# A four-layer image kernel: in layer 0, the first two turns of a block's attention weights are issued directly behind the next block's scores

## The chip, the cores and the metric

The kernel runs on one core of a Trainium2 chip. The core has five engines that work at the same time, each through its own list of instructions: TensorE (PE in the profile, with its weight loads shown apart as PEld), VectorE (DVE), ScalarE (ACT), GpSimd (POOL) and SyncE (SP), which here only issues DMAs. The metric is the device time of one execution in microseconds, lower is better; the median of three runs before the change is 3686.7 us (3686.67 to 3689.1).

## The reference

Four layers follow each other on 4 images of 64 x 64 points with 128 channels, in 32-bit floats. Layer 0, the only one that is touched, is neighbourhood attention: every point attends, in 4 heads of 32 channels, to the 7 x 7 points around it (shifted inward at the borders), with a learned bias for each relative place. The result is projected, multiplied by a gate that is computed from the input, and added to the input.

```python
qkv = (x @ qkv_w + qkv_b).reshape(B, H, W, 3, HEADS, HEAD_DIM)
q = qkv[..., 0, :, :] * HEAD_DIM ** (-0.5)
...
scores = jnp.einsum('bxyhd,bxyklhd->bxyhkl', q, kwin) + bias[None]
attn = jax.nn.softmax(scores.reshape(B, H, W, HEADS, k * k), axis=-1)
...
out = jnp.einsum('bxyhkl,bxyklhd->bxyhd', attn, vwin).reshape(B, H, W, C)
return out @ proj_w + proj_b
...
gate = jax.nn.sigmoid(jax.nn.relu(x @ g1_w + g1_b) @ g2_w + g2_b)
return attn_out * gate + x
```

Layer 1 is a group normalisation with full attention over the 4096 points, layer 2 a gated product with a layer normalisation, layer 3 a convolution with a selective scan in four directions. None of them is changed.

## The kernel before, in words

The images go through layers 0 to 2 one after the other (the loop over b at L1134). For each image the generator `layer_0` (L359) runs its whole loop before `layer_1` starts, since layer 1 begins with statistics over the image; only its first eight steps (the first two chunks of the intake) are taken during layer 1 of the image before. Layer 3 follows at the end.

An image is cut into 32 blocks (NT) of 8 x 16 points, that is 128 points each. The keys that a block can reach are a rectangle of up to 14 x 22 points: nk is 14 x 19 = 266 for the blocks at the left and right border and 14 x 22 = 308 for the others, or 209 and 242 in the first and the last row of blocks. A block goes through these steps, each a small function:

- `score(i)` (L448): SP loads the block's values; TensorE multiplies queries and keys, one matmul for each head (L477, 32 rows of the array each), into four banks of PSUM. VectorE adds the bias and takes the maximum, head by head (L481), and turns the sign of the maxima (L484). Then `bias_in(i)` (L438) lets GpSimd add the projection's bias times the gate to the block's input (L441, L442).
- `soften(i, heads)` (L490): ScalarE takes the exponential of two heads and their sums (L495).
- `normalise(i)` (L499): VectorE takes the reciprocal of the four sums (L501), GpSimd multiplies the weights of each head by it, in place (L503).
- `by_key(i, g, evac)` (L506): TensorE turns one third of the block's weights so that the keys stand on the partitions: one transpose for each head (L512) into one PSUM bank with the tag "t", and one engine copies the bank to SBUF (L514). Thirds 0 and 2 are copied by ScalarE, third 1 by VectorE. Border blocks of the first and the last row have two parts instead of three.
- `value(i)` (L517): TensorE multiplies the turned weights with the values, a matmul for each third and head (L523, 32 columns of the array each); ScalarE copies the result (L528).
- `project(i)` (L530): TensorE multiplies with the projection's weights (L533); VectorE multiplies by the gate and adds to the input (L534).

Three other things are spread over the loop. `take_in(n, part)` (L377) is the intake of a chunk of four blocks: part 0 finishes the gate of the chunk before (L424 to L426) and turns the input (L387, copied at L389), part 1 computes the queries (L393, L394), part 2 the keys (L400, L401), part 3 values and gate (L411 to L420). `hand_on(n)` (L428) turns four finished blocks for layer 1, also through a bank with the tag "t" (L432), and ScalarE copies it (L433). `statistics(n)` (L435) follows one iteration later on VectorE. "t" has two banks, which are taken in turn by the thirds of `by_key`, by part 0 of the intake and by `hand_on`.

The loop (L543) is a software pipeline: one iteration i issues the scores of block i+3, the values of block i-1, the normalising of block i+1, the projection of block i-2, the turns of block i and the exponentials of block i+2. Instructions that stand in `pin(...)` keep their written order on their engine; those are all of TensorE, VectorE and ScalarE in this loop. The GpSimd operations (L441, L442, L503) and the loads of values on SP are not pinned: their place in their engine's list is set by the planner, which puts there what its plan finds ready first. In the trace the four `bias_in` of a chunk run together on GpSimd, as soon as that chunk's gate is ready.

Of the kernel before, what the change touches and what calls it, by code (L numbers as in the profile page):

```python
# [32 lines left out]
NT = L // P  # L33
# [105 lines left out]
def layers_0_to_2(  # L139
    ctx, tc, xf, mata, matb, rows, rpb, convw, sel, ident, cl, dram, big, ring, early, x3_d, ub_d, zf_d, y_d, dbl_d, ct_d, gw_d, bw_d  # L140
):
    nc = tc.nc
# [10 lines left out]
    def ps_t(shape, name):  # L153
        return psp.tile(shape, F32, name=name, tag="t", bufs=2)
# [31 lines left out]
    def load_x(b, xt=None, tiles=(0, NT), queue=nc.sync, kept=False):  # L186
        if xt is None:
            xt = ring([P, NT, C], f"x_{b}")
        src = xf[b].rearrange("(r w) c -> r w c", w=W)
        for j in range(*tiles):  # L190
            r, c = BR * (j // 4), BC * (j % 4)
            ins = queue.dma_start(xt[:, j, :], src[r:r + BR, c:c + BC, :])
            if kept:

                tc.keep_in_program_order(ins)
        return xt
# [162 lines left out]
    def layer_0(b, xt, edge_t):  # L359
# [12 lines left out]
        def pin(ins):  # L372
            return tc.keep_in_program_order(ins)
# [54 lines left out]
        def hand_on(n):  # L428

            pt = ps_t([P, 4, P], "pt")  # L430
            for k in range(4):
                pin(nc.tensor.transpose(pt[:, k, :], xt[:, 4 * n + k, :], ident))  # L432
            pin(nc.scalar.copy(hT[:, bass.ts(n, CH)], pt.rearrange("p k t -> p (k t)")))  # L433

        def statistics(n):  # L435
            pin(nc.vector.bn_stats(st[:, n, :], hT[:, bass.ts(n, CH)]))
# [53 lines left out]
        def soften(i, heads):  # L490
            k = blocks[i]
            if heads[0] == 0:
                k.sm = sml.tile([P, HEADS], F32, name="sm0", tag="sm0", bufs=4)
            for h in heads:
                pin(nc.scalar.activation(  # L495
                    k.pr[:, h], k.pr[:, h], AF.Exp, bias=k.mx[:, h:h + 1], accum_out=k.sm[:, h:h + 1]
                ))

        def normalise(i):  # L499
            k = blocks[i]  # L500
            pin(nc.vector.reciprocal(k.sm, k.sm))  # L501
            for h in range(HEADS):
                nc.gpsimd.tensor_scalar(k.pr[:, h], k.pr[:, h], k.sm[:, h:h + 1], 1.0, ALU.mult, ALU.mult)  # L503
            k.prT = []

        def by_key(i, g, evac):  # L506
            k = blocks[i]
            if g < len(k.tiles):
                at, n, _ = k.tiles[g]
                pt = ps_t([P, HEADS, P], "pt0")  # L510
                for h in range(HEADS):
                    pin(nc.tensor.transpose(pt[0:n, h, :], k.pr[:, h, at:at + n], ident))  # L512
                prT = tmp.tile([P, HEADS, P], F32, name="prT0", tag="c512", bufs=9)
                pin(evac(prT[0:n], pt[0:n]))  # L514
                k.prT.append(prT)

        def value(i):  # L517
            k = blocks[i]
            po = ps_o([P, P], "po0")
            for g, (at, n, slot) in enumerate(k.tiles):  # L520
                for h in range(HEADS):
                    hp = slice(HD * h, HD * h + HD)
                    pin(nc.tensor.matmul(  # L523
                        po[hp, :], lhsT=vs[0:n, slot, hp], rhs=k.prT[g][0:n, h, :],
                        start=(g == 0), stop=(g == len(k.tiles) - 1),
                    ))
            k.oT = tmp.tile([P, P], F32, name="oT0", tag="oT")
            pin(nc.scalar.copy(k.oT, po))  # L528

        def project(i):  # L530
            k = blocks.pop(i)
            pp = ps_o([P, C], "pp0")
            pin(nc.tensor.matmul(pp, lhsT=k.oT, rhs=m("proj"), start=True, stop=True))  # L533
            pin(nc.vector.scalar_tensor_tensor(xt[:, i, :], pp, gate[:, i:i + 1], xt[:, i, :], ALU.mult, ALU.add))  # L534
# [8 lines left out]
        for i in range(-3, NT + 5):  # L543
            if i + 3 < NT:
                score(i + 3)
            if b == 0 and i < 1:
                load_x(0, xt, (4 * i + 28, 4 * i + 32), kept=True)
            if 0 <= i - 1 < NT:
                value(i - 1)
            if 0 <= i + 1 < NT:  # L550
                normalise(i + 1)
            if 0 <= i - 2 < NT:
                project(i - 2)
            if 0 <= i < NT:
                by_key(i, 0, nc.scalar.copy)
                by_key(i, 1, nc.vector.tensor_copy)
            if 0 <= i + 2 < NT:
                soften(i + 2, (0, 1))
            n, part = divmod(i + 3, 4)
            if n + 2 < NCH or (n + 2, part) == (NCH, 0):  # L560
                take_in(n + 2, part)
            if 0 <= i < NT:
                by_key(i, 2, nc.scalar.copy)
            if 0 <= i + 2 < NT:
                soften(i + 2, (2, 3))

            n, part = divmod(i - 6, 4)
            if 0 <= n < NCH and part == 0:
                hand_on(n)
            if 0 <= n < NCH and part == (1 if n < NCH - 1 else 0):  # L570
                statistics(n)
# [211 lines left out]
    def front(b):  # L783
# [343 lines left out]
        return turn  # L1127

    coming = layer_0(0, x_next, edge_of[0])
    for _ in range(8):  # L1130
        next(coming)
    weights()
    ahead = [x_next]
    for b in range(B):  # L1134
# [26 lines left out]
        if b + 1 < B:  # L1161
            coming = layer_0(b + 1, ahead[0], edge_of[b + 1])
# [385 lines left out]
```

## Time and profile before

| | before |
|---|---|
| median of three runs | 3686.7 us |
| the profiled execution | 3685.77 us |
| its span, first to last instruction | 3684.0 us, mean granted clock 0.920 |
| busy over the span: PE, PEld, DVE, ACT, POOL | 3322.1, 2753.6, 2834.4, 2677.1, 1419.6 us |
| scores of layer 0 (L477), by image | 25.0 to 179.1, 768.9 to 898.9, 1513.2 to 1643.1, 2257.4 to 2387.5 us |
| turns (L512), mean of a matmul, count | 276 ns, 1472 |
| values (L523), mean of a matmul, count | 278 ns, 2944 |
| copies of turned thirds (L514) | ScalarE 240 of 578 ns, VectorE 128 of 686 ns |
| normalising (L503) | 512 of 495 ns on GpSimd |
| exponentials (L495) | 512 of 517 ns on ScalarE |

A group's line in the profile gives line, engine, operation, written and read tiles, shapes, and then busy time, mean duration, and the idle time of the engine just before, with what ended it. In a timeline a row is a run of equal instructions: its start, its length, the engine, and in square brackets the idle time before it and what ended that. "issue" stands for time in which the engine waited for nothing that the profile shows. Times in a timeline are microseconds from the start of the span. Layer 0's loops take about 600 us of the 3684; the rest belongs to the other layers.

### The profile page before, as it was taken

Reading aid. Unit: us, or ns where it says so; the run is one execution under the profiler, and the core shown is the slowest. Engines: PE = TensorE matmul, PEld = TensorE weight load, DVE = VectorE, ACT = ScalarE, POOL = GpSimd, SP = SyncE. Lnnn points to the kernel's source line nnn. Section 1 sums busy time; section 2 is a strip of 40 time slices with the busy share of each in tenths; the row PEclk is TensorE's granted clock in tenths of the full one; section 3 lists DMA queues with packets and bytes.
Section 4 is the critical chain, followed back from the end, with each engine's and each line's share of the span. In section 5 each row is a group of like instructions: output and inputs, shape, how many; then the busy total and the mean of one; then the engine's idle time right before and its main releaser. Section 6 shows DMA issues by size and latency. Waiting matters only on the chain. (4 is left out here: it accounts for less than half of the span.)

```text
span 3684.0 us, 69605 instructions
## 1 busy us (share of the span) xinstructions
PE 3322.1 (90%) x26458; PEld 2753.6 (75%) x26458; DVE 2834.4 (77%) x5325; ACT 2677.1 (73%) x4355; POOL 1419.6 (39%) x1592
## 2 busy tenths in 40 slices
PE   7999999999999999999999999989999997666647
PEld 4679999966899999667999996679999962222236
DVE  5757878767678788776777886767878768999968
ACT  4855677777676777786777777866777769999934
POOL 6500011245122122451222223512222338999866
PEclk8999999999999999999999999999999995555579
DMA  4200000131010012410121213100101269999998
GB/s 123 73 4 28 9 18 33 55 96 31 18 48 29 33 46 84 132 36 18 44 67 33 76 54 94 39 1 27 44 28 35 67 186 236 217 232 212 209 277 283
DMA packets 189394, 310.91 MB, mean 84 GB/s; under 512 B 23007, under 2 KB 111996, under 8 KB 184156
## 3 DMA queue, kind: packets, MB, share of 16 engines
q1 hardware_dynamic: 146260, 220.27, 17.8%
q0 software_dynamic: 24384, 76.95, 11.7%
q10 hardware_dynamic: 18416, 9.24, 0.9%
q8 instruction: 208, 3.41, 0.4%
q14 instruction: 126, 1.03, 0.1%
HBM read 167.69 MB, written 155.56 MB: 88 GB/s over the span
## 5 line engine op out<-in xcount | busy, mean ns | idle before, releaser
L634 PE MATMUL sc<-qT,kT 128*128 128x128 f32 x8192 | 1084.2, 276 | 15.6 <-DVE mx L640 15.6
L667 PE MATMUL po<-v,st 128*128 128x129 f32 x8192 | 1082.1, 275 | 2.0 <-ACT st L661 2.0
L634 PEld LDWEIGHTS sc<-qT,kT 128*128 128x128 f32 x8192 | 1001.4, 193 | 38.4 <-issue 26.6
L667 PEld LDWEIGHTS po<-v,st 128*128 128x128 f32 x8192 | 999.6, 192 | 4.7 <-ACT st L661 2.2
L637 ACT COPY st<-sc 128x512 f32<-128x512 f32 x1024 | 574.0, 583 | 426.9 <-PE sc L634 425.9
L640 DVE TENSOR_TENSOR mx<-mx,sc 128x512 f32<-128x512 f32 x768 | 524.0, 682 | 202.8 <-ACT st L637 178.7
L660 DVE TENSOR_TENSOR st<-st,pb 128x2048 f32<-128x2048 f32 x256 | 574.5, 2280 | 4.8 <-PE pb L657 3.7
L661 ACT ACTIVATE st<-st 128x2048 f32<-128x2048 f32 x256 | 483.1, 1908 | 64.5 <-DVE st L660 63.8
L1258 PE MATMUL pdt<-dbl,dt 8*128 8x512 f32 x512 | 307.2, 1079 | 142.6 <-ACT de L1265 141.8
L1269 POOL TENSOR_TENSOR inp<-de,ub 128x1024 f32<-128x1024 f32 x128 | 409.9, 4399 | 9.3 <-DMA ub_d<-u 5.1
L1258 PEld LDWEIGHTS pdt<-dbl,dt 8*128 8x128 f32 x512 | 114.0, 311 | 332.9 <-ACT de L1265 270.0
L503 POOL TENSOR_SCALAR pr<-pr,sm 128x308 f32<-128x308 f32 (+3 forms) x512 | 243.7, 495 | 206.2 <-DVE sm L501 187.9
L733 POOL TENSOR_TENSOR x<-x,row 128x512 f32<-128x512 f32 x32 | 40.8, 1275 | 696.1 <-PE pt L295 696.1
L879 POOL TENSOR_TENSOR gsum<-gsum,tp 128x504 f32<-128x504 f32 (+1 forms) x177 | 240.9, 1364 | 170.7 <-ACT tp L871 84.1
L495 ACT ACTIVATE pr<-pr,mx 128x308 f32<-128x308 f32 (+3 forms) x512 | 262.8, 517 | 1.3 <-DVE mx L484 1.3
L1296 DVE TENSOR_TENSOR_SCAN h<-h,end,inp 128x1024 f32<-128x1024 f32 x96 | 221.1, 2346 | 18.7 <-ACT h L1282 8.1
L512 PE MATMUL pt<-ident,pr 128*88 128x128 f32 (+5 forms) x1472 | 205.5, 276 | 10.2 <-ACT prT L514 8.8
L1311 POOL DMA_DIRECT2D y<-yo x112 | 201.1, 2719 | 10.7 <-DVE yo L1310 7.6
L888 DVE SCALAR_TENSOR_TENSOR acc<-xh,cc,acc 128x512 f32<-128x512 f32 (+3 forms) x250 | 199.8, 820 | 4.6 <-ACT acc L852 3.6
L512 PEld LDWEIGHTS pt<-ident,pr 128*88 128x88 f32 (+5 forms) x1472 | 164.6, 138 | 45.8 <-ACT prT L514 25.9
L481 DVE CUSTOM_DVE_ANT_0 pr<-sc,bias_m 128x266 f32<-128x266 f32 (+1 forms) x384 | 152.1, 452 | 57.8 <-PE sc L477 57.0
L514 ACT COPY prT<-pt 110x512 f32<-110x512 f32 (+3 forms) x240 | 138.8, 578 | 70.5 <-PE pt L512 69.3
(234 smaller groups left out, 5132.1 us busy)
## 6 DMA issues: line engine op xcount, KB each, us to landing
y<-yo POOLq DMA_DIRECT2D x112, 512.0 KB, 10.6
y<-y SPq DMA_DIRECT2D x48, 512.0 KB
zf_d<-zf SPq DMA_DIRECT2D x64, 256.0 KB
ub_d<-u SPq DMA_DIRECT2D x64, 256.0 KB
ub<-ub_d SPq DMA_DIRECT2D x16, 1024.0 KB
yl<-y SPq DMA_DIRECT2D x64, 256.0 KB
zc<-zf_d SPq DMA_DIRECT2D x64, 256.0 KB
v_d<-vg SPq DMA_DIRECT2D x128, 64.0 KB
```

Of the source, the lines that this page charges most:

```text
L495: pin(nc.scalar.activation(k.pr[:, h], k.pr[:, h], AF.Exp, bias=k.mx[:, h:h + 1], accum_out=k.sm[:, h:h + 1]))
L503: nc.gpsimd.tensor_scalar(k.pr[:, h], k.pr[:, h], k.sm[:, h:h + 1], 1.0, ALU.mult, ALU.mult)
L512: pin(nc.tensor.transpose(pt[0:n, h, :], k.pr[:, h, at:at + n], ident))
L634: nc.tensor.matmul(ps[:, r, :], lhsT=kT[:, bass.ts(G * g + r, P)], rhs=qT[:, bass.ts(i, P)], start=True, stop=True)
L637: nc.scalar.copy(k.st[:, G * g:G * g + G, :], ps)
L640: nc.vector.tensor_tensor(k.mx, k.st[:, 0:G, :] if g == 1 else k.mx, ps, ALU.max)
L660: nc.vector.tensor_tensor(part, part, pb.unsqueeze(1).to_broadcast([P, 16, P]), ALU.add)
L661: nc.scalar.activation(part, part, AF.Exp)
L667: nc.tensor.matmul(k.po, lhsT=k.st[:, j, :], rhs=v[:, j, :], start=(j == 0), stop=(j == NT - 1))
L879: nc.gpsimd.tensor_tensor(a, a, p, ALU.add)
L1258: nc.tensor.matmul(pdt[j][:, g, :], lhsT=dt[o:o + RANK, P * f:P * f + P], rhs=at(dbl[o:o + RANK, :], k & 2, g0, g0 + CH), start=True, stop ...
L1269: nc.gpsimd.tensor_tensor(by_rows(inp), by_rows(de), at(ub_s[f], b ^ (k & 1), SC * n, SC * n + SC), ALU.mult)
```

## The change

In the loop of `layer_0`, the two calls that turn thirds 0 and 1 of block i move up: they now stand directly behind the scores of block i+3 (and, for image 0, behind the loads of input), ahead of the values of block i-1, the normalising of block i+1 and the projection of block i-2. The turn of the last third stays where it is, behind the intake. Functions, tiles and numbers of buffers are the same.

```diff
                 score(i + 3)
             if b == 0 and i < 1:
                 load_x(0, xt, (4 * i + 28, 4 * i + 32), kept=True)
+            if 0 <= i < NT:
+                by_key(i, 0, nc.scalar.copy)
+                by_key(i, 1, nc.vector.tensor_copy)
             if 0 <= i - 1 < NT:
                 value(i - 1)
             if 0 <= i + 1 < NT:
                 normalise(i + 1)
             if 0 <= i - 2 < NT:
                 project(i - 2)
-            if 0 <= i < NT:
-                by_key(i, 0, nc.scalar.copy)
-                by_key(i, 1, nc.vector.tensor_copy)
             if 0 <= i + 2 < NT:
                 soften(i + 2, (0, 1))
```

On TensorE an iteration was: scores, values, projection, turns 0 and 1, intake, turn 2, `hand_on`. It becomes: scores, turns 0 and 1, values, projection, intake, turn 2, `hand_on`. On ScalarE the copy of turn 0 now comes ahead of the copy of the values' result; on VectorE the copy of turn 1 now comes ahead of the reciprocal and of the projection's result.

## The prediction

> **What bounds the kernel now.** The change touches only layer 0's loop over 32 blocks, which runs once for each of four images. So I first took busy times by stretch, for a regular piece of image 1 (four blocks, from scores 12 to scores 16, then scores 16 to 20).
>
> ```profile
> core 0: us, PE busy (x) PEld busy (x) DVE busy (x) ACT busy (x) POOL busy (x), PEclk, DMA share, GB/s
> 816.46:834.82 18.36, 18.12 (x206) 13.19 (x205) 14.35 (x56) 15.80 (x49) 10.88 (x24) 1.00 0.18 49
> 834.82:853.18 18.36, 18.12 (x206) 13.19 (x205) 14.35 (x56) 15.79 (x49) 10.87 (x24) 1.00 0.17 49
> ```
>
> Four blocks take 18.36 us, twice the same. TensorE shows 18.12 us busy, ScalarE 15.8, VectorE 14.35, GpSimd 10.9, the granted clock is 1.00. TensorE comes first, but its busy time contains pipelined ends, so I next read the timeline of its weight loads for one block and the waits of the stretch.
>
> ```profile
> 834.82 0.58 PEld L477 LDWEIGHTS sc<-kT,qT 32*128 32x128 f32 x8 [0.19 <-issue]
> 835.74 0.60 PEld L523 LDWEIGHTS po<-prT,v 95*32 95x32 f32 x24 [0.35 <-issue]
> 836.53 0.30 PEld L533 LDWEIGHTS pp<-ma,oT 128*128 128x128 f32 x2 [0.20 <-issue]
> 836.75 0.90 PEld L512 LDWEIGHTS pt<-ident,pr 128*110 128x110 f32 x8
> 838.13 0.42 PEld L387 LDWEIGHTS pt<-ident,x 128*128 128x128 f32 x4 [0.48 <-ACT prT L514]
> 838.68 0.38 PEld L512 LDWEIGHTS pt<-ident,pr 128*88 128x88 f32 x4
> 839.25 0.31 PEld L477 LDWEIGHTS sc<-kT,qT 32*128 32x128 f32 x8 [0.18 <-issue]
> ```
>
> Call the pieces S (scores, L477), V (values, L523), P (projection, L533), T0 and T1 (the two turns that move; one row of 8 loads), T2 (third turn). The wait that the change can remove is the 0.48: the two "t" banks hold T0 and T1, and the next turn needs ScalarE's copy of T0. It comes in iterations with an x turn (take_in part 0) and in those without a matmul of the intake. The rest are gaps of 0.2 to 0.4 us, between S, V and P.
>
> Then GpSimd and VectorE, whose work decides when T0 may start:
>
> ```profile
> 837.41 0.17 DVE L484 TENSOR_SCALAR mx<-mx 128x4 f32<-128x4 f32 x1
> 837.48 0.18 DVE L501 RECIPROCAL sm<-sm 128x4 f32<-128x4 f32 x1
> 837.58 0.32 DVE L534 SCALAR_TENSOR_TENSOR x<-pp,gate,x 128x128 f32<-128x128 f32 x1
> 837.94 0.69 DVE L514 COPY prT<-pt 110x512 f32<-110x512 f32 x1
> ```
>
> ```profile
> 837.76 2.01 POOL L503 TENSOR_SCALAR pr<-pr,sm 128x308 f32<-128x308 f32 x4 [3.41 <-DVE sm L501]
> 840.17 0.72 POOL L441 TENSOR_SCALAR gb<-row,gate 128x128 f32<-128x128 f32 x2 [0.40 <-DVE gate L426]
> 840.85 0.87 POOL L442 TENSOR_TENSOR x<-x,gb 128x128 f32<-128x128 f32 x2
> ...
> 843.22 1.90 POOL L503 TENSOR_SCALAR pr<-pr,sm 128x266 f32<-128x266 f32 x4
> ```
>
> GpSimd normalises block 14 until 839.77 and its T0 starts at 840.99: 1.2 us of slack. Once in four blocks the four bias_in (3.05 us) stand between, and block 15 is ready at 845.12 for a T0 at 845.68. These slacks are what the move spends.
>
> **The change part by part.** Nothing is added or removed. Of each block 16 loads and matmuls (8 each), one ScalarE copy and one VectorE copy move ahead of V (16 or 24 pairs, one ScalarE copy), normalise (one VectorE reciprocal, four GpSimd multiplications) and P (two pairs, one VectorE operation). No DMA moves, so SP's queue keeps its order; on GpSimd the order stays, only its cause comes later.
>
> (1) *Gaps on TensorE.* S to V was 0.35 (0.42 where S has 308 columns). S to T0 is seen once in each image's start, V after a turn at the end:
>
> ```profile
> 777.54 0.89 PEld L512 LDWEIGHTS pt<-ident,pr 128*114 128x114 f32 x8 [0.25 <-POOL pr L503]
> 904.68 0.38 PEld L523 LDWEIGHTS po<-prT,v 88*32 88x32 f32 x16 [0.20 <-issue]
> ```
>
> The 0.25 followed scores of 209 columns, the same as S to V has there, so I let S to T0 cost what S to V cost; the 0.20 is new, once a block. Bounds: 0 (P to T0 showed no gap) and 0.25. [...]
>
> (2) *The 0.48 wait.* T2 or the x turn now comes 0.65+0.79+0.22 us behind T1, longer than ScalarE's copy of T0 takes (0.75 from T0's start until it begins, then 0.58). It goes: -0.48 in part 0 and in the last third. [...]
>
> (3) *A new chain.* On VectorE the reciprocal for block i+1 now stands behind the copy of T1 of block i, on GpSimd the normalising behind it, and T0 of block i+1 behind that. Behind the waiting copy also stand the P result and the intake's operations. Steps: T1's first load to the copy 0.73 (832.45 to 833.18, where it waited), copy to next operation 0.66 (833.18 to 833.84), reciprocal to GpSimd 0.27 (837.48 to 837.76), four multiplications 1.90 or 2.01, the fourth to T0's last head and T1 0.17. Together 3.73 to 3.84 us per block from T1 to T1. Without intake a block takes about 3.6 now (P to P 3.62, 3.52, 3.58 from block 21 on), so there this chain is the slower one.
>
> (4) *The bank of the hT turn.* In one of four iterations hand_on turns x behind T2, and ScalarE copies it last (826.92 to 827.49). T1 of the next block needs that bank. It came at 827.77, 0.28 later; now T1 comes about 1 us earlier in its iteration and waits.
>
> Laid out for four iterations, from S of part 0 at 0, each piece at the latest of its causes, with S to T0 0.92, 0.73, 0.87 as measured, V 0.65 behind T1, P 0.79 behind V, the next piece 0.22 behind P, then 1.12, 1.93, 1.50, 1.94 to the next S:
> Part 0: T0 0.92, V 2.02, S 4.15; VectorE is free for the copy at 2.67, so reciprocal 3.33, GpSimd 3.60 to 5.61, bias_in to 8.66.
> Part 1: S 4.15; T0 could start at 4.88, its fourth head waits until 5.67, T1 5.78 (0.45 late); V 6.43, P 7.22, S 9.37. VectorE has the gate until 5.35, then the four reductions, copy 7.15, reciprocal 7.81; GpSimd 8.66 to 10.56. ScalarE: copy of T0 6.40, oT behind V 7.42, two exponentials, qT, T2's copy, two exponentials, hT 10.73 to 11.30.
> Part 2: T0 10.24, fourth head 10.62, T1 waits for hT until 11.33 (0.64 late); V 11.98, S 14.49. kT from ScalarE ends 14.97.
> Part 3: T0 15.66 (S waits for kT, 0.13 less than before), next S 19.71.
> So 19.71 instead of 18.36: **+1.35 per four blocks**. In the first four no hT stands: T1 at 10.73, next S at 19.14 against 18.22, +0.92.
> The last third, from scores 24 (871.53) to the last projection (912.39), takes 40.86 now. By the same steps, 3.7 to 3.8 per block and two more hT waits (about 0.1 and 1.05), the last projection comes at 44.3: **+3.4**.
> Per image 0.92 + 4 x 1.35 + 3.4 = 9.7. Image 0 waits for its input in the first blocks (P to P up to 9.14), which hides a little: 9. Sum 3 x 9.7 + 9 = **+38 us**.
>
> The profiled execution took 3685.77 us (span 3684.0 and 1.8 around it), 0.9 below the median of 3686.7. 3685.8 + 38 = **3724 us**. Layer 0's loop ends before layer 1 starts (statistics of the whole image), so its loss is not hidden. Apart from (1) and (2), which make 6.2 paid and 10.1 saved an image (worked out under the first rival), the sum holds 9.7 + 3.9 = 13.6 us of new waits an image. Half of them would give 3697, half again as many 3751; a gap of 0 or 0.25 in (1) moves 3724 to 3699 or 3730.
>
> **Rivals.** *Faster: the chain stays inside its slack.* Then TensorE alone counts: 31 x 0.20 = 6.2 paid, 16 x 0.48 + 3 x 0.5 (hT turn waiting for VectorE's copy) + 0.9 (V waiting for T2's copy at the end) = 10.1 saved, -3.9 an image: 3670; with no gap behind T1, 3646. For it: part 0 and part 3 have 2.4 and 1.8 us of slack. Against: 1.2 and 0.55 in the two others.
> *No change: only the bank of hT bites.* 0.72 six times an image, 4.3, against 3.9 saved: 3687. It needs GpSimd to be on time everywhere, which the last third speaks against, as bias_in is hardly there and the chain alone takes 3.7.
> *Much slower: GpSimd's order turns.* Normalising is not pinned; if bias_in (3.05 us) came ahead of a due normalising in each group, the 3.05 less the 0.45 of part 1 would be lost, 2.6 x 6 x 4 = 62 more: 3786. Against: the gate that releases bias_in follows the reciprocal on VectorE.
> That the change doesn't do what it says: on TensorE, ScalarE and VectorE the order is pinned, so it must show.
>
> **How the numbers follow.** Forecast 0.80, faster 0.09, no change 0.07, much slower 0.04. A difference under 0.2% (7 us) can't be told from none. So slower 0.84, within 0.07, faster 0.09. The range takes in the halved and the enlarged waits and reaches towards no change: 3695 to 3757.
>
> **What would show it.** P to P without intake at 3.7 to 3.8 instead of 3.5 to 3.6; four-block groups at 19.7; the reciprocal directly behind VectorE's copy; T0 or T1 waiting for GpSimd L503 and, behind hT, for ScalarE L433; V 0.2 behind T1; no wait before the x turn; layer 1 and later as long as before. Wrong would be T0 never waiting for GpSimd (then 3670), or a group longer than 20.5.

## The result, and the profile after

The changed kernel takes 3714.5 us (median of 4 runs, 3713.08 to 3718.77) against 3687.9 us for the kernel before (4 runs, 3686.67 to 3693.69). The ratio is 1.0072, with a 95% interval of 1.0059 to 1.0084: slower by 27 us, where the forecast was slower by 38 (3724, range 3695 to 3757). The profiled execution's span went from 3684.0 to 3711.3 us, at the same mean granted clock of 0.920.

First the groups of instructions that the change touches, before and after (busy time and mean of one, then the idle time just before them and what ended most of it). Before:

```profile
L503 POOL TENSOR_SCALAR pr<-pr,sm 128x308 f32<-128x308 f32 (+3 forms) x512 | 243.7, 495 | 206.2 <-DVE sm L501 187.9
...
L512 PEld LDWEIGHTS pt<-ident,pr 128*88 128x88 f32 (+5 forms) x1472 | 164.6, 138 | 45.8 <-ACT prT L514 25.9
...
L523 PEld LDWEIGHTS po<-prT,v 95*32 95x32 f32 (+5 forms) x2944 | 71.9, 110 | 55.4 <-issue 39.8 <-DMA v<-v_d 5.8 <-ACT prT L514 5.4
```

After:

```profile
L503 POOL TENSOR_SCALAR pr<-pr,sm 128x308 f32<-128x308 f32 (+3 forms) x512 | 245.3, 498 | 246.9 <-DVE sm L501 216.6
...
L512 PEld LDWEIGHTS pt<-ident,pr 128*88 128x88 f32 (+5 forms) x1472 | 164.1, 138 | 120.8 <-POOL pr L503 68.2
...
L523 PEld LDWEIGHTS po<-prT,v 95*32 95x32 f32 (+5 forms) x2944 | 73.6, 110 | 21.8 <-issue 11.0 <-ACT oT L528 0.8 <-DMA v<-v_d 0.7
```

Neither operation became slower (495 and 498 ns, 138 and 138 ns). What changed is who waits for whom. Before, the turns' loads (L512) waited 45.8 us in all, more than half of it for ScalarE's copies of earlier turns (a bank). After, they wait 120.8 us, 68.2 of it put down to GpSimd's normalising. Not all of this is new: the loads of the values (L523) wait 33.6 us less (55.4 to 21.8), because the gap behind the scores now stands ahead of the turns. Together the two groups wait 41 us more. GpSimd itself waits 40.7 us more, 28.7 of it put down to VectorE's reciprocal. These sums fit the chain of term (3); the timelines and the runs below have to show it.

Then where the time lies. From the timeline of TensorE's loads I took, for each image, the time from scores 0 to the last projection, and from scores 24 to the last projection:

| us | image 0 | image 1 | image 2 | image 3 |
|---|---|---|---|---|
| layer 0's loop, before | 167.64 | 143.47 | 143.43 | 143.66 |
| after | 170.69 | 151.99 | 151.27 | 151.91 |
| difference | +3.05 | +8.52 | +7.84 | +8.25 |
| of it the last third | +3.05 | +3.60 | +3.06 | +3.67 |

The four differences add up to 27.7 us, all of the loss; the other layers together take what they took. Two regular groups of image 1 after the change, by busy time in stretches, from scores 12 and from scores 16:

```profile
core 0: us, PE busy (x) PEld busy (x) DVE busy (x) ACT busy (x) POOL busy (x), PEclk, DMA share, GB/s
821.11:840.68 19.57, 19.03 (x205) 13.14 (x204) 14.24 (x56) 15.72 (x49) 11.02 (x25) 1.00 0.16 46
840.68:860.04 19.36, 18.82 (x205) 13.15 (x204) 14.16 (x56) 15.62 (x49) 10.77 (x25) 1.00 0.16 45
```

Four blocks that took 18.36 us now take 19.4 to 19.6, with the same work on each engine and the clock at 1.00. TensorE's busy time grew with the span, from 18.12 to about 19, although no matmul was added: its busy share is no help here. The timeline of the weight loads over three iterations of the second group is:

```profile
840.68 0.58 PEld L477 LDWEIGHTS sc<-kT,qT 32*128 32x128 f32 x8 [0.19 <-issue]
841.61 0.84 PEld L512 LDWEIGHTS pt<-ident,pr 128*110 128x110 f32 x8 [0.35 <-issue]
842.62 0.60 PEld L523 LDWEIGHTS po<-prT,v 95*32 95x32 f32 x24 [0.17 <-issue]
843.42 0.30 PEld L533 LDWEIGHTS pp<-ma,oT 128*128 128x128 f32 x2 [0.20 <-issue]
843.64 0.47 PEld L387 LDWEIGHTS pt<-ident,x 128*128 128x128 f32 x4
...
844.71 0.31 PEld L477 LDWEIGHTS sc<-kT,qT 32*128 32x128 f32 x8 [0.19 <-issue]
845.66 0.30 PEld L512 LDWEIGHTS pt<-ident,pr 128*110 128x110 f32 x3 [0.63 <-POOL pr L503]
846.29 0.51 PEld L512 LDWEIGHTS pt<-ident,pr 128*110 128x110 f32 x5 [0.34 <-POOL pr L503]
...
850.66 0.35 PEld L512 LDWEIGHTS pt<-ident,pr 128*95 128x95 f32 x3 [0.42 <-POOL pr L503]
851.25 0.16 PEld L512 LDWEIGHTS pt<-ident,pr 128*95 128x95 f32 x1 [0.24 <-POOL pr L503]
851.85 0.46 PEld L512 LDWEIGHTS pt<-ident,pr 128*95 128x95 f32 x4 [0.44 <-ACT hT L433]
```

Part 0 (first five rows) shows the gain that the move has: T0 follows S, V follows T1 by 0.17, and the x turn (L387) starts without the 0.48 of before. Part 1 pays: T0's row is broken, three heads and then five, since the fourth head is not normalised yet. In part 2 T0 is broken again, and T1 (the last row) waits 0.44 for ScalarE's copy L433, which frees the bank of the hT turn: term (4). A row in which all eight loads stand together and that shows 0.35 or 0.42 is another matter: that is what S to V cost before, too, whatever name is put to it.

GpSimd and VectorE ahead of the broken row at 845.66:

```profile
843.28 0.17 DVE L484 TENSOR_SCALAR mx<-mx 128x4 f32<-128x4 f32 x1
843.35 0.69 DVE L514 COPY prT<-pt 110x512 f32<-110x512 f32 x1
843.95 0.17 DVE L501 RECIPROCAL sm<-sm 128x4 f32<-128x4 f32 x1
```

```profile
844.22 2.02 POOL L503 TENSOR_SCALAR pr<-pr,sm 128x308 f32<-128x308 f32 x4 [3.49 <-DVE sm L501]
```

The reciprocal, which stood directly behind L484, has the copy of T1 in front of it. GpSimd starts 0.27 behind it and ends at 846.24; the fourth head's load starts at 846.29.

### The profile page after: what moved, and what is told of

It is laid out like the page before. It is cut to its first block, busy times and chain, and to the rows that moved or that the text cites. A ratio compares the mean times of both kernels' runs of the same rounds, so it can differ in the third digit from the quotient of the medians.

```text
span 3711.3 us, 69435 instructions
## 1 busy us (share of the span) xinstructions
PE 3345.1 (90%) x26458; PEld 2754.6 (74%) x26458; DVE 2833.5 (76%) x5325; ACT 2676.0 (72%) x4355; POOL 1422.6 (38%) x1592
## 5 line engine op out<-in xcount | busy, mean ns | idle before, releaser
L512 PE MATMUL pt<-ident,pr 128*88 128x128 f32 (+5 forms) x1472 | 236.5, 285 | 26.4 <-POOL pr L503 6.7
L512 PEld LDWEIGHTS pt<-ident,pr 128*88 128x88 f32 (+5 forms) x1472 | 164.1, 138 | 120.8 <-POOL pr L503 68.2
L481 DVE CUSTOM_DVE_ANT_0 pr<-sc,bias_m 128x266 f32<-128x266 f32 (+1 forms) x384 | 151.9, 452 | 68.4 <-PE sc L477 66.6
L729 POOL TENSOR_TENSOR o<-o,rt 128x512 f32<-128x512 f32 x32 | 34.3, 1072 | 360.2 <-DVE o L728 360.2
```

## The experiments

Nine kernels ran, with the kernel before beside them on the same chip. S to S is measured in a regular four-block group of image 1, parts 0 to 3; "last third" is scores 24 to the last projection there. The medians of the kernel before beside them were 3686.2 (the first four), 3687.9 (turn0_alone, projection_behind and the two late edges) and 3685.8 (best_two). Where the texts put on record speak of tiled matmuls, they mean S and V, whose loads have 32 rows or 32 columns; a switch is a step between one of them and a piece whose loads have 128 rows and 66 columns or more. The rows of the regular groups show how long the gap there is (V to P 0.20 us, the last turn to S 0.17 to 0.19, T1 to V 0.14 to 0.18, S to T0 0.35 or 0.42 as S to V), not what makes it.

| kernel | median us | ratio to before, 95% | parts 0, 1, 2, 3 | last third | images 0, 1, 2, 3 |
|---|---|---|---|---|---|
| before | | | 4.43, 4.55, 4.25, 5.13 | 40.86 | 167.6, 143.5, 143.4, 143.7 |
| after | 3714.5 | 1.0072 (1.0059 to 1.0084) | 4.03, 5.22, 5.04, 5.08 | 44.46 | 170.7, 152.0, 151.3, 151.9 |
| reciprocal_first | 3699.0 | 1.0033 (1.0021 to 1.0045) | 4.05, 4.89, 5.03, 5.08 | 41.31 | 165.8, 146.9, 146.7, 146.8 |
| other_bank | 3703.3 | 1.0051 (1.0036 to 1.0066) | 4.03, 5.20, 4.53, 5.08 | 43.13 | 166.4, 148.5, 148.3, 148.4 |
| both_undone | 3683.9 | 0.9988 (0.9979 to 0.9998) | 4.05, 4.89, 4.29, 5.08 | 40.09 | 163.7, 142.8, 142.6, 142.6 |
| control_bank | 3695.2 | 1.0027 (1.0017 to 1.0037) | 4.43, 4.55, 4.70, 5.13 | 40.91 | 166.3, 145.4, 145.4, 145.6 |
| turn0_alone | 3697.2 | 1.0027 (1.0016 to 1.0038) | 4.58, 5.03, 4.29, 5.05 | 41.51 | 167.7, 146.5, 145.8, 146.5 |
| projection_behind | 3663.6 | 0.9937 (0.9920 to 0.9954) | 4.16, 4.50, 4.09, 4.88 | 38.32 | 161.4, 137.4, 137.4, 138.2 |
| before_late_edge | 3680.4 | 0.9982 (0.9973 to 0.9991) | | | 162.1, others 143.4 to 143.5 |
| after_late_edge | 3713.7 | 1.0074 (1.0059 to 1.0089) | | | 169.4, others 151.1 |
| best_two | 3662.9 | 0.9937 (0.9923 to 0.9950) | | | image 0: 156.0 |

**The chain alone taken away** (reciprocal_first): the changed kernel, with the reciprocal ahead of the copy of T1 on VectorE. TensorE's order is that of the changed kernel.

```diff
+            if 0 <= i + 1 < NT:
+                normalise(i + 1)
             if 0 <= i < NT:
                 by_key(i, 0, nc.scalar.copy)
                 by_key(i, 1, nc.vector.tensor_copy)
             if 0 <= i - 1 < NT:
                 value(i - 1)
-            if 0 <= i + 1 < NT:
-                normalise(i + 1)
```

> The changed kernel, but normalise(i+1) stands ahead of the two moved turns, so VectorE takes the reciprocal before it copies turn 1. Theory (two waits: the chain copy, reciprocal, GpSimd, turn; and the bank of the hT turn): the chain goes, T0 of part 1 no longer waits for GpSimd, the hT bank wait stays but comes 0.45 us earlier; four blocks take about 19.0 instead of 19.4 us, the last third about 42 instead of 44.2, in all about 3697 us (3692 to 3702). Rival (the loss is the extra switch between tiled and untiled matmuls, 31 x 4 x 0.2 = 25 us, and the waits are only where slack is spent): unchanged at 3714.

3699.0 us, as expected. Part 1 fell by 0.33 and the last third by 3.15; images 1 to 3 became 4.9 us shorter each (in the mean, 151.7 to 146.8). On VectorE the reciprocal stands behind L484 again:

```profile
838.42 0.17 DVE L484 TENSOR_SCALAR mx<-mx 128x4 f32<-128x4 f32 x1
838.50 0.18 DVE L501 RECIPROCAL sm<-sm 128x4 f32<-128x4 f32 x1
838.60 0.66 DVE L514 COPY prT<-pt 110x512 f32<-110x512 f32 x1
```

Part 2 stayed at 5.03, and there the loads of T0 and T1 show the other term by itself, larger than in the changed kernel, since T0 no longer hides a share of it:

```profile
845.50 0.47 PEld L512 LDWEIGHTS pt<-ident,pr 128*95 128x95 f32 x4 [0.42 <-POOL pr L503]
846.68 0.46 PEld L512 LDWEIGHTS pt<-ident,pr 128*95 128x95 f32 x4 [0.72 <-ACT hT L433]
```

**The bank alone taken away** (other_bank): the changed kernel, with the hT turn in a bank with the tag "o" (where the results of V and P lie) instead of "t".

```diff
         def hand_on(n):
-            pt = ps_t([P, 4, P], "pt")
+            pt = ps_o([P, 4, P], "pt")
```

> The changed kernel, but the hT turn of hand_on writes one of the two banks with the tag o (values and projection) instead of t. Theory: the wait of turn 1 behind ScalarE's hT copy goes, some 0.5 us in four groups an image and about 1.1 us twice in the last third, 3 to 3.5 us an image, so about 3700 to 3703 us; the GpSimd waits stay. Rival of the switches: unchanged at 3714.

3703.3 us, at the edge of what was expected. Part 2 fell by 0.51, no other part by more than 0.02, the last third by 1.33; images 1 to 3 became 3.3 us shorter each. In part 2 the fourth head of T0 still waits for GpSimd, but T1 follows it in the same row, without a wait for hT:

```profile
846.67 0.35 PEld L512 LDWEIGHTS pt<-ident,pr 128*95 128x95 f32 x3 [0.42 <-POOL pr L503]
847.24 0.57 PEld L512 LDWEIGHTS pt<-ident,pr 128*95 128x95 f32 x5 [0.22 <-POOL pr L503]
```

**Both taken away** (both_undone): both edits together. What is left of the change is TensorE's order.

> Both edits together: reciprocal ahead of the turns, hT in a bank of tag o. Theory: only the TensorE terms are left, 6.2 us of switches paid and about 10 us of waits saved an image, so 3672 to 3682 us, below the kernel before. Rival of the switches: 3714.

3683.9 us. The loss is gone: the interval ends below 1, if hardly. Images 1 to 3 became 9.05 us shorter each, against 4.93 + 3.33 = 8.26 for the two alone, so the terms nearly add and neither replaced the other. The rival of the switches, for which the whole loss is one more change between tiled and untiled matmuls, is out: that change is still there, and the loss is not. In the four loops of the profiled executions the two edits took away 19.7 and 14.3 us, each by itself, and 34.1 together; the medians fell by 15.5, 11.2 and 30.6. The executions also differ by some us outside of these loops, so the shares are read from the loops. But the gain of TensorE alone, 3.9 us an image, isn't there: 142.7 against 143.5 is 0.85. One reason stands in the last third, in the loads of T0:

```profile
877.17 0.16 PEld L512 LDWEIGHTS pt<-ident,pr 128*95 128x95 f32 x1 [0.47 <-POOL pr L503]
877.64 0.16 PEld L512 LDWEIGHTS pt<-ident,pr 128*95 128x95 f32 x1 [0.31 <-POOL pr L503]
878.11 0.16 PEld L512 LDWEIGHTS pt<-ident,pr 128*95 128x95 f32 x1 [0.31 <-POOL pr L503]
878.58 0.57 PEld L512 LDWEIGHTS pt<-ident,pr 128*95 128x95 f32 x5 [0.31 <-POOL pr L503]
```

One load each 0.47 us is GpSimd's pace (1.90 for four heads): T0 runs as fast as GpSimd normalises. The waits inside T0's and the later turns' rows add up to 3.7 us in this last third, where the kernel before has none for GpSimd. Moving T0 about 1 us ahead uses up GpSimd's slack even with the reciprocal as early as before.

**The bank edit on the kernel before** (control_bank), to see that it is neutral by itself.

> The kernel before, with the hT turn in a bank of tag o. Both theories: 3688 us, within 3 of the kernel before, since turn 1 came 0.28 us behind the free bank there. If it were faster by several us, the bank would have been a limit already and the other_bank run would prove less.

It isn't neutral: 3695.2 us, 9 slower. The load of P in part 2 shows a part of it:

```profile
846.59 0.30 PEld L533 LDWEIGHTS pp<-ma,oT 128*128 128x128 f32 x2 [0.65 <-ACT hT L433]
```

Now P needs the bank that hT occupies, and in the kernel before it comes too early for that. Part 2 becomes 0.45 us longer and images 1 to 3 take 1.9 us more each, but image 0 takes 1.4 less: that is 4.4 us in the four loops. The rest of the 9 us lies outside of them, and no run shows its cause. In the changed order T0 and T1 stand between S and V, so P comes about 1 us later in its iteration, by when the bank is free: neither other_bank nor both_undone has such a wait. Inside the loops the edit is a fix for the changed kernel only; what other_bank took away it took away there, so its reading of the loops stands.

**Only T0 moved** (turn0_alone): T1 stays behind the projection, so the reciprocal keeps its place and T1 its bank.

```diff
                 score(i + 3)
+            if 0 <= i < NT:
+                by_key(i, 0, nc.scalar.copy)
...
                 project(i - 2)
-            if 0 <= i < NT:
-                by_key(i, 0, nc.scalar.copy)
-                by_key(i, 1, nc.vector.tensor_copy)
+            if 0 <= i < NT: by_key(i, 1, nc.vector.tensor_copy)
```

> Only turn 0 stands behind the scores; turn 1 stays behind the projection. VectorE's order is that of before (reciprocal ahead of the copy of turn 1), and turn 1 comes late enough for hT's bank. The switch between tiled and untiled matmuls is paid as in the changed kernel. Theory: neither wait comes, so about the time of both_undone, 3680 to 3688 us, four blocks 18.3 to 18.6 us. Rival of the switches: 31 x 4 x 0.2 = 25 us are lost here too, so about 3712.

3697.2 us, in neither theory's range. The x turn has its bank, but T2 and the hT turn don't:

```profile
838.92 0.47 PEld L387 LDWEIGHTS pt<-ident,x 128*128 128x128 f32 x4
839.98 0.38 PEld L512 LDWEIGHTS pt<-ident,pr 128*88 128x88 f32 x4 [0.59 <-DVE prT L514]
...
844.97 0.42 PEld L432 LDWEIGHTS pt<-ident,x 128*128 128x128 f32 x4 [0.36 <-DVE prT L514]
```

The two banks are taken in turn. With T0's bank free early, the x turn takes it at once, and the next user asks for T1's bank, whose copy on VectorE isn't done: the 0.48 before the x turn became 0.59 behind it. A wait for one bank of a ring was moved to the ring's next user, with interest.

**The projection moved instead of the turns** (projection_behind): the kernel before, with P behind T0 and T1. If the 0.48 is a matter of 0.2 to 0.5 us of work between T1 and the next turn, P fills it, and V, reciprocal, T0 and T1 keep their order.

```diff
-            if 0 <= i - 2 < NT:
-                project(i - 2)
             if 0 <= i < NT:
                 by_key(i, 0, nc.scalar.copy)
                 by_key(i, 1, nc.vector.tensor_copy)
+            if 0 <= i - 2 < NT:
+                project(i - 2)
```

> The kernel before with project(i-2) moved behind the two turns: scores, values, turns 0 and 1, projection. One switch fewer is not gained, but turns come 0.22 us earlier and the projection's 0.22 us fills part of the 0.48 us wait before the x turn (part 0) and before turn 2 (last third). Theory (waits for banks, not engine work, set these stretches): part 0 falls from 4.43 to about 4.2 us, the last third by 0.22 a block, some 16 x 0.22 = 3.5 us an image, so 3672 to 3676 us. Rival: ScalarE is the bound there and nothing moves, 3686.

3663.6 us: faster than the kernel before by 0.6%, and more than expected. Its loads in part 0:

```profile
829.19 0.60 PEld L523 LDWEIGHTS po<-prT,v 95*32 95x32 f32 x24 [0.35 <-issue]
829.99 0.84 PEld L512 LDWEIGHTS pt<-ident,pr 128*110 128x110 f32 x8 [0.20 <-issue]
830.80 0.30 PEld L533 LDWEIGHTS pp<-ma,oT 128*128 128x128 f32 x2
831.31 0.42 PEld L387 LDWEIGHTS pt<-ident,x 128*128 128x128 f32 x4 [0.21 <-ACT prT L514]
```

P fills the time in which ScalarE copies T0, the wait falls from 0.48 to 0.21, and there is no additional gap: V to T0 costs the 0.20 that V to P cost, T1 to P shows none. A four-block group takes 17.63 us instead of 18.36. Of this 0.73 only 0.27 lies in part 0. Part 3 gave 0.25; there the kernel before has S waiting in the middle, for the keys that ScalarE copies (L401), and this kernel does not:

```profile
848.05 0.31 PEld L477 LDWEIGHTS sc<-kT,qT 32*128 32x128 f32 x6 [0.19 <-issue]
848.71 0.29 PEld L477 LDWEIGHTS sc<-kT,qT 32*128 32x128 f32 x2 [0.35 <-ACT kT L401]
```

That is a reading of the two timelines. No run took that wait away by itself. Of the 0.16 of part 2, 0.14 lies between S and V (0.73 us instead of 0.87), and its cause isn't shown.

**The edge's loads moved** (before_late_edge, after_late_edge): image 0 lost only 3.05 us where the others lost 8.2. In the kernel before TensorE stands still there for 3.46 us, waiting for the values of block 8, whose DMAs come behind the loads of an edge's bias on SP's queue (issued from 77.98 to 85.63 us). Both kernels were run with these loads at block 20.

```diff
-            if i == 7:
+            if i == 20:
                 edges[2] = edge_bias(2)
```

> The kernel before with edge_bias(2) built at block 20 instead of 7, so that its DMAs on SP don't stand ahead of the value loads of blocks 8 and on in image 0. Theory for the mis-sized term (image 0 hides part of the loss because in the kernel before its values of block 8 wait 3.5 us for their DMA and TensorE's clock falls behind that): image 0 gets some 4 to 7 us shorter, so 3680 to 3683 us. Rival (image 0's blocks are simply slower for another reason): unchanged, 3686.

> The changed kernel with the same edit. Theory: image 0 has no such wait here, so it stays within 2 us of the changed kernel, 3712 to 3715 us, and the distance to before_late_edge grows from 27 to about 32 us, close to four times the 8.2 of images 1 to 3. Rival: the distance stays 27.

As expected: the kernel before gains (3680.4, image 0 by 5.5 us), the changed one hardly (3713.7, image 0 by 1.3), and their distance is 33.3 us instead of 27. With this wait out of the way image 0 loses 169.4 - 162.1 = 7.3, nearly as much as the others: the DMA wait had hidden most of the loss.

**Both improvements together** (best_two): projection_behind with the late edge.

> Both edits that made the kernel before faster: project(i-2) behind the turns (3663.6) and edge_bias(2) at block 20 instead of 7 (5.5 us less in image 0 there). Theory: they act in different images' stretches, image 0 still shows 8.7 us more between scores 4 and 24 than the others in projection_behind, so another 5 to 6 us go: 3657 to 3660 us. Rival: with shorter blocks image 0 waits for its loads anyway: 3663.

3662.9 us (3657.32 to 3664.44 over 5 runs). In its profiled execution image 0 takes 156.0 us, 5.4 less than with projection_behind alone, and that execution took 3657.3. But the medians differ by only 0.7 us, less than the runs differ among each other: whether the late edge brings anything on top isn't settled.

## Why the prediction was right, and where its sizes were off

**Direction and cause held.** The chain (3) and the bank (4) are the loss: with both taken away it is gone (both_undone), each alone takes its share (4.9 and 3.3 us an image), and the rows that were named show them. In the last third the chain's period can be read directly, from copy of T1 to copy of T1 on VectorE:

```profile
894.78 0.68 DVE L514 COPY prT<-pt 95x512 f32<-95x512 f32 x1
...
898.51 0.69 DVE L514 COPY prT<-pt 110x512 f32<-110x512 f32 x1 [0.25 <-PE pt L512]
...
902.28 0.68 DVE L514 COPY prT<-pt 110x512 f32<-110x512 f32 x1
```

That is 3.73 and 3.77 us, for the 3.73 to 3.84 that were added up from five rows of the kernel before.

**That the total came so near is in part luck.** The sum held 13.6 us of new waits an image and 3.9 us of gain by TensorE's order. In images 1 to 3, both_undone against the changed kernel has 9.05 for the first, and against the kernel before 0.85 for the second. The waits were taken 4.5 too long and the gain 3.1 too large, and in 9.7 against the measured 8.2 the two errors mostly cancel.

**The groups were laid out well.** Predicted 4.15, 5.22, 5.12, 5.22; measured 4.03, 5.22, 5.04, 5.08. The broken T0 in part 1 and the T1 behind hT in part 2 came where they were placed. In image 1 the mean of the full groups grew by 1.08 instead of 1.35, the first four blocks by 0.61 instead of 0.92. The wait for hT was 0.44 rather than 0.64. The last third, predicted at +3.4, took +3.05 to +3.67. So images 1 to 3 lost 8.2 each instead of 9.7.

**Image 0 was the term mis-sized most**, 9 predicted and 3.05 measured. "Hides a little" was taken from the gaps between projections and priced at 0.7; what V waits for in these gaps wasn't followed. The stretch from 91 to 101 us of the kernel before, busy times and its row of V:

```profile
91.00:101.00 10.00, 6.96 (x52) 4.58 (x52) 3.95 (x17) 3.88 (x14) 2.50 (x6) 0.69 0.39 127
```

```profile
94.85 0.20 PEld L523 LDWEIGHTS po<-prT,v 95*32 95x32 f32 x8 [3.46 <-DMA v<-v_d]
...
96.84 1.71 PEld L512 LDWEIGHTS pt<-ident,pr 128*110 128x110 f32 x8
```

And of the changed kernel:

```profile
91.00:101.00 10.00, 9.78 (x115) 7.16 (x108) 8.17 (x33) 7.84 (x26) 6.26 (x15) 1.00 0.43 142
```

The kernel before waits 3.46 us for a transfer, and its granted clock over the stretch is 0.69. In the changed one the same scores come 2.9 us later (93.23 instead of 90.35) and V stands behind two turns, at 95.17, when the values have landed; the clock stays at 1.00. What had been lost up to there cost nothing. Part of that is image 0's own: in its second group T0 waits 2.19 us, until 58.20, for GpSimd, which issues ten DMAs of an edge's bias (52.53 to 57.64) ahead of the normalising, and the granted clock is 0.50 from 60.3 to 63.6. This group took 2.05 us longer, against 0.61 in image 1. A loss that comes ahead of a wait for DMA is paid out of that wait first. The two late edges confirm it with 33 us of distance. Of the 11 us that the forecast was too long, 6 are image 0 and 3 x 1.5 the others.

**The gaps (1)** were right: V stands 0.14 to 0.18 behind T1 where 0.20 was taken. The row stands behind that, and the runs agree in both directions: the changed order has one change between tiled and untiled matmuls more in each block and pays 0.17, projection_behind keeps their number and pays none. What makes the gap isn't shown.

**The wait saved (2)** was right in its place (no wait before the x turn) but not in its net value. With (3) and (4) taken away, TensorE alone should have brought 3.9 us an image; it brought 0.85. In the full groups the sum erred the other way: four gaps of 0.2 less one wait of 0.48 make 0.3 more, and both_undone's groups take 18.31 us, 0.05 less than before, since from S to the next piece parts 2 and 3 take 0.73 and 1.09 us instead of 0.87 and 1.30. The gain is missing in the last third. I had added up gaps and waits on TensorE as though GpSimd had only the chain to fear. It also has less time: T0 is asked for about 1 us earlier in each block, and in the last third that alone makes it wait 3.7 us inside its rows. The "faster" rival named the slacks of 1.2 and 0.55 us as what speaks against it, but its 3670 had no price for using them up, so this order doesn't reach it even without the chain.

**The rivals.** "No change, only hT's bank bites" is out: the chain cost more than the bank. "Much slower, GpSimd's order turns" is out: the order of GpSimd's instructions is the same, except that one DMA of an edge's bias comes ahead of four multiplications at image 0's start. That the change might not do what it says is out by the timeline. The gap of 0.48 us was a wait for a bank; no run gave the turns a third one, but asking for the same two banks in another order (this change, turn0_alone) gave the wait to another turn, and filling the gap with work that needs neither bank (projection_behind) gained 24 us.

## What to carry to other kernels

Before work is moved ahead to fill a gap on the busiest engine, follow what its results are queued in front of on the other engines: a copy that moves ahead of a small reciprocal can close a loop over three engines. Move the piece whose result is needed last: here P, which only the later hT turn reads, fills the same gap for nothing. And price an expected loss in each stretch against the waits for DMA that stand behind it, as they swallow it.

## What the runs showed of the hardware that was not expected

After the 3.46 us in which TensorE waited for the values of block 8, the eight loads of a turn took 1.71 us where they take 0.84 to 0.90 elsewhere, and the granted clock was 0.69 over the 10 us from 91 (0.50 from 94.8 to 101.5); in the changed kernel, without that wait, it was 1.00 over the same 10 us. What sets the clock isn't shown, and a single wait as long as 3.46 us doesn't stand ahead of every fall: the changed kernel's 0.50 from 60.3 to 63.6 came when TensorE had been busy for 1.88 of the 4 us from 56 to 60, with no wait longer than 2.19. The wait of 3.46 us cost more than itself: with the late edge V waits 0.35 us there instead of 3.46 and the clock of that stretch is 1.00, and image 0 became 5.5 us shorter.
